# Cross-attention and FP4 feed-forward layer on one core: twenty loads of x issued by GpSimd instead of SyncE

## The chip, the core and the metric

One core of a Trainium2 chip runs the whole layer as one program. The metric is the device time of the program in microseconds (us), the median of several executions. The engines are called as the profile calls them: PE (TensorE), DVE (VectorE), ACT (ScalarE), POOL (GpSimd) and SP (SyncE, which here does nothing but issue DMA transfers). Each engine works through its own instructions in the order in which the program gives them; an instruction that has to wait for a semaphore holds up everything behind it on that engine.

## What is computed

The input `x` has 4 batches of 2048 rows of 512 numbers in float32; the context has 4 batches of 77 rows. Cut to what matters:

```python
def layer(x, ctx, mask, Wq, bq, Wk, bk, Wv, bv, Wo, bo, w_gate, w_up, w_down):
    x = x + attention(layernorm(x), ctx, ctx, mask, Wq, bq, Wk, bk, Wv, bv, Wo, bo)   # 16 heads of 32
    return x + ffn(layernorm(x), w_gate, w_up, w_down)

def ffn(x, w_gate, w_up, w_down):                    # widths 512 -> 1408 -> 512
    h = silu(fp4_linear(x, w_gate)) * fp4_linear(x, w_up)
    return fp4_linear(h, w_down)

def fp4_linear(x, w):                                # both operands rounded to 4-bit floats,
    return fp4(x) @ fp4(w).T                         # with one scale for each block of 16 numbers
```

The kernel does each product in float16 with two parts (high and low) of each operand, in three passes.

## The kernel before

The 8192 rows of `x` are worked on in 64 tiles of 128 rows. Before the tiles can run at full rate, the weights have to be loaded, scaled, rounded (gate, up and down weights: steps `wg0` to `wd3`) or split into two parts (attention weights, by PE products with scaled diagonals into PSUM and two ACT copies: steps `pk0` to `po3`), and keys and values of the context have to be made. Steps of the first tiles are woven into that preparation.

Every piece of work is a generator that yields its steps in order, and an emission order over all these steps is written out by hand in the string `INTRO` (the preparation and about the first eighteen tiles); after it a list of due times (`PLACE`) orders the steps, and a string `OUTRO` ends it. A word such as `at.8` in the string means "the next step of the attention of tile 8"; `at.2*2` means the next two. The order of the words is the order of the instructions on every engine. Moving an instruction to another engine does not change the string: the instruction keeps its place among all steps and so gets a new place among that engine's instructions.

Each tile `t` loads its 128 rows of `x` twice, 256 KB each time:

- `xin`, at line 875, the first step of `attention(t)`. There are two buffers, so the load of tile `t` waits until tile `t - 2` has been read for the last time, by DVE at line 887. The next steps of the tile are: moments of the rows on DVE (lines 845 and 847), five small POOL operations for the reciprocal standard deviation and a sixth for the bias `nb` (lines 853 to 860, 881), the normalised rows and their high part on ACT (883, 885), the low part on DVE (887), a transposing DMA (890), the query product on PE.
- `x`, at line 867, the first step of `residual(t)`; POOL then adds the output bias (869), and DVE adds the attention's output (1004). There are five buffers; at first some of them hold raw context and values of the preparation, later a buffer comes free when the tile that had it five tiles ago has been stored (1138).

Later steps of the attention that are named below: scores on PE (917), their masking and row maxima on DVE (928, 937), the negated maxima `nmx` on POOL (940), sixteen exponentials on ACT (944), the split of the probabilities on ACT and DVE (947, 949), a transposing DMA of them to `pT` (952), the product with the values on PE (969), its scaling on DVE (984, 987), a transposing DMA to `aT` (997), the output product on PE (1000). The feed-forward part of a tile follows with its products `gps`, `ups` and `dps`.

All DMA transfers of the kernel, loads, stores and transposes, are issued by SP, through one queue (q1 on the profile's page). The words of the order that surround five of the loads:

```
... sg at.0*3 pc0*4 dk pk1*2 v*3 dv pv2*2 pv1*2 pv2*2 pk1*2 at.1*3 pv0*2 wg0 wu2 wu1*2 ...
... wd2*3 wu3 sd*2 at.6*2 at.8 at.2*2 wd1 sd wd2 sd*2 wd1*2 at.0 ...
... at.1*2 r.1 at.0 gu.0 at.8 at.9*2 at.1*2 x.2 ...
```

In the first of these lines `at.0*3` is the load of tile 0, its moments on DVE and its six POOL operations; `dk` and `dv` (line 406, DVE) make the scaled diagonals that PE needs for the parts of Wk (`pk`) and Wv (`pv`). In the second, `sd` are scales of the down weights (line 757 on POOL, 781 on ACT, 784 on DVE), `at.6*2` is ACT's and DVE's preparation of tile 6 (883, 885, 887), `at.8` is the load of tile 8, and `at.2*2` is `nmx` of tile 2 on POOL and the first four of its exponentials. In the third, `r.1` are five POOL operations of tile 1 (line 1036), and `at.9*2` is the load of tile 9 and its moments.

Of the kernel before, what the change touches and what calls it, by code (L numbers as in the profile page):

```python
# [91 lines left out]
    x=(7.3299, 8.0685,),  # L92
    r=(8.1990,),
# [13 lines left out]
def step(e, take=(), give=(), wait=(), fire=(), on=False):  # L107


    return e, take, give, wait, fire, on  # L110
# [63 lines left out]
def tile_xattn_fp4_ffn(  # L174
# [18 lines left out]
    nc = tc.nc  # L193
# [3 lines left out]
    H, DK, P, Q = 16, 32, 128, 16  # L197
# [4 lines left out]
    ST = S // P  # L202
# [11 lines left out]
        x=5, xin=2, xhl=1, xT=2, qst=1, sc=1, pT=2, an=1, ahl=1, aT=1, xc=1, xqhl=1, xqT=2, sg=2, hh=2, ah=2, hqhl=1, hT=1, ax=1  # L214
    )

    def buf(tag, shape, dt, name=None):
        return wk.tile([P] + list(shape), dt, tag=tag, name=name or tag, bufs=BUFS[tag])
# [631 lines left out]
    def rstd(mv, k, f):  # L850
# [9 lines left out]
        nc.gpsimd.tensor_scalar(rs, e, r0, None, ALU.mult)  # L860
        return rs

    def residual(t):
        b, r = divmod(t, ST)
        yield step("D", take=[("x", t)], wait=[("vf", NB - 1)])
        xt = tiles["x", t] = buf("x", [D], F32)
        nc.sync.dma_start(xt, x[b].rearrange("(p t) d -> p t d", p=P)[:, r])
        yield step("G", wait=["bo"], fire=[("x", t)])
        nc.gpsimd.tensor_tensor(xt, xt, bo_sb, ALU.add)

    def attention(t):
        b, r = divmod(t, ST)
        yield step("D", take=[("xin", t)])
        xt = buf("xin", [D], F32)
        nc.sync.dma_start(xt, x[b].rearrange("(p t) d -> p t d", p=P)[:, r])
        yield step("V")
        mv = moments(xt, "1")
        yield step("G")
# [124 lines left out]
        xt = tiles["x", t]  # L1003
# [185 lines left out]
    def spawn(order):  # L1189
        while ("done", ended[0]) in order.events:  # L1190
            ended[0] += 1
        while begun[0] < min(N, ended[0] + AHEAD):
            t = begun[0]
            begun[0] += 1
            if t and t % ST == 0:
                order.add("kb", t, batch_keys(t // ST))
                order.add("vb", t, batch_values(t // ST))
            order.add("at", t, attention(t))
            order.add("x", t, residual(t))
            order.add("gu", t, gateup(t))  # L1200
            order.add("s", t, gates(t))
            order.add("r", t, second_rstd(t))
            order.add("px", t, scales_x(t))
            order.add("ph", t, scales_h(t))
            order.add("h", t, hidden(t))
        return begun[0] < N
# [43 lines left out]
```

## Time and profile before

| | |
|---|---|
| time, median of 3 runs | 2003.44 us (2000.14 to 2004.87) |
| the profiled execution's own time | 2004.46 us |
| its span, first to last instruction | 2002.7 us |
| busy: PE, DVE, ACT, POOL | 1892.5, 1714.4, 1385.5, 917.0 us |
| queue q1, all DMA transfers | 250.72 MB, 62.2% of 16 engines' span |
| issue of an `xin` load on SP, shortest, median, longest | 0.328, 0.571, 1.584 us |
| issue of an `x` load on SP, shortest, median, longest | 0.327, 0.328, 0.577 us |

In the views quoted below, an engine's row gives the start in us from the beginning of the span, the duration in us, the engine, the line of the kernel, the operation, what it writes and reads, shape and count, and in brackets the idle time of the engine before it with what ended it. "SPq" is an issue on SP: its duration is the time of the issue, not of the transfer. "PEclk" is the share of the full TensorE clock that was granted.

### The profile page before, as it was taken

What the parts mean: (1) busy time and instruction counts of PE and PEld (TensorE: products, weight loads), DVE (VectorE), ACT (ScalarE), POOL (GpSimd) and SP (SyncE); (2) the same over time, 40 slices, a digit from 0 to 9 for tenths busy, and PEclk for the clock granted to TensorE, in tenths of its full rate; (3) what the DMA queues carried; (4) which work ended last, traced back from release to release, by engine and by line L of the source; (5) the groups of instructions that cost most, each with busy time, mean ns of one, the idle gap of its engine ahead of it and who ended that gap; (6) DMA issues with size and microseconds to landing.
All of it is one profiled execution on the core that took longest, in us unless ns stands there. A gap on an engine that the chain in (4) does not pass through costs nothing.

```text
span 2002.7 us, 32553 instructions
## 1 busy us (share of the span) xinstructions
PE 1892.5 (94%) x11834; PEld 972.3 (49%) x11834; DVE 1714.4 (86%) x2810; ACT 1385.5 (69%) x2263; POOL 917.0 (46%) x1210
## 2 busy tenths in 40 slices
PE   2744999999999999999999999999999999999997
PEld 1622555555555555555555555555555555555543
DVE  7788988888888888898888888888889888888874
ACT  5867877667766777667766776677766776677531
POOL 4335345444444445544454445444454445444531
PEclk9866999999999999999999999999999999999999
DMA  8479676656656656665666575665765566656431
GB/s 251 91 198 206 105 136 127 130 120 125 133 121 131 122 122 125 132 120 121 129 129 118 123 130 119 132 126 116 135 131 114 120 128 128 119 117 114 88 76 45
DMA packets 778553, 252.80 MB, mean 126 GB/s; under 512 B 738292, under 2 KB 749684, under 8 KB 778391
## 3 DMA queue, kind: packets, MB, share of 16 engines
q1 hardware_dynamic: 778391, 250.72, 62.2%
q8 instruction: 92, 1.51, 0.3%
q14 instruction: 70, 0.57, 0.1%
HBM read 52.11 MB, written 17.92 MB: 35 GB/s over the span
## 4 chain that ended last, share of the span: by engine, by line
PE 88%; DVE 4%; ACT 3%; DMA 2%; POOL 1%; issue 1%; SPq 0%; DVEq 0%; POOLq 0%
PE dps L385 22%; PE gps L385 22%; PE ups L385 22%; PE ops L385 8%; PE qps L385 8%; PE avps L969 3%; PE scps L917 2%; PE wps L416 1%; ACT sc L944 1%; DMA hT<-hqhl 1%; DMA pT<-ph 1%; DMA wuT<-in_L_ffn_w_up_dram 0%; DVE wam L377 0%; DVE wsc L710 0%; DMA wdT<-wraw 0%
## 5 line engine op out<-in xcount | busy, mean ns | idle before, releaser
L385 PEld LDWEIGHTS <-xqT 128*128 128x128 f16 x4608 | 447.1, 98 | 453.9
L385 PE MATMUL ups<-wuT,xqT 128*128 128x512 f16 (+1 forms) x2304 | 487.8, 361 | 0.0
L385 PE MATMUL gps<-wgT,xqT 128*128 128x512 f16 (+1 forms) x2304 | 487.7, 361 | 0.0
L385 PE MATMUL dps<-wdT,hT 128*128 128x512 f16 x2112 | 468.4, 380 | 6.3 <-DMA hT<-hqhl 6.2
L944 ACT ACTIVATE sc<-sc,nmx,cells 128x77 f32<-128x77 f32 x1024 | 363.2, 438 | 8.6 <-POOL nmx L940 7.9
L385 PEld LDWEIGHTS <-hT 128*128 128x128 f16 x2112 | 206.8, 98 | 257.5 <-DMA hT<-hqhl 7.7
L1093 ACT ACTIVATE sg<-gps,cells 128x512 f32<-128x512 f32 (+1 forms) x192 | 123.8, 646 | 137.6 <-PE gps L385 133.0
L853 POOL TENSOR_SCALAR ve<-mv 128x1 f32<-128x1 f32 x128 | 111.1, 868 | 235.4 <-DVE mv L847 229.6
L385 PE MATMUL ops<-woT,aT 128*128 128x512 f16 x768 | 179.8, 384 | 17.3 <-DMA aT<-ahl 9.6
L704 POOL TENSOR_TENSOR hh<-hh,rh 128x1408 f32<-128x1408 f32 x64 | 165.7, 2589 | 42.8 <-DVE rh L764 42.3
L898 ACT ACTIVATE q<-qps 128x1024 f16<-128x1024 f32 x64 | 65.3, 1021 | 171.3 <-PE qps L385 171.3
L385 PE MATMUL qps<-wqT,xT 128*128 128x512 f16 x768 | 182.3, 389 | 0.0
L949 DVE TENSOR_TENSOR ph<-sc,ph 128x1232 f16<-128x1232 f32 x64 | 151.3, 2363 | 32.7 <-ACT ph L947 32.6
L883 ACT ACTIVATE xin<-xin,nb,rs 128x512 f32<-128x512 f32 x64 | 52.0, 813 | 173.5 <-POOL nb L881 173.5
L855 POOL TENSOR_TENSOR r<-ve,nhalf 128x1 f32<-128x1 f32 x128 | 153.5, 1199 | 10.7
L1103 DVE SCALAR_TENSOR_TENSOR hh<-ups,cells,sg 128x512 f32<-128x512 f32 (+1 forms) x192 | 128.5, 670 | 17.0 <-PE ups L385 15.3
L1069 POOL TENSOR_SCALAR cd<-pw,cells 128x1 f32<-128x1 f32 x64 | 18.3, 285 | 252.7 <-DVE pw L1066 252.7
L704 POOL TENSOR_TENSOR xc<-xc,rix 128x512 f32<-128x512 f32 x64 | 67.7, 1058 | 135.8 <-DVE rix L1020 130.3
L757 POOL TENSOR_SCALAR sh<-amh 128x88 f32<-128x88 f32 x64 | 33.3, 520 | 196.0 <-DVE amh L377 195.9
L385 PEld LDWEIGHTS <-xT 128*128 128x128 f16 x768 | 76.3, 100 | 87.5 <-issue 7.5
L385 PEld LDWEIGHTS <-aT 128*128 128x128 f16 x768 | 71.7, 99 | 96.6 <-DMA aT<-ahl 15.0
L857 POOL TENSOR_SCALAR e<-ve,r 128x1 f32<-128x1 f32 x128 | 102.7, 802 | 14.7
(190 smaller groups left out, 3023.3 us busy)
## 6 DMA issues: line engine op xcount, KB each, us to landing
xin<-in_x_dram SPq DMA_DIRECT2D x64, 256.0 KB
x<-in_x_dram SPq DMA_DIRECT2D x64, 256.0 KB
out_dram<-x SPq DMA_DIRECT2D x64, 256.0 KB
wgT<-in_L_ffn_w_gate_dram SPq DMA_DIRECT2D x4, 704.0 KB
wuT<-in_L_ffn_w_up_dram SPq DMA_DIRECT2D x4, 704.0 KB
wmraw<-in_L_ffn_w_down_dram SPq DMA_DIRECT2D x4, 704.0 KB
wraw<-in_L_ffn_w_down_dram SPq DMA_DIRECT2D x4, 704.0 KB
wqT<-in_L_xattn_Wk_dram SPq DMA_DIRECT2D x4, 256.0 KB
```

Source lines behind the costliest of these rows:

```text
L385: nc.tensor.matmul(o, lhs(a, c), rhs(b, c), start=(k == 0), stop=(k == 3 * n - 1))
L704: nc.gpsimd.tensor_tensor(dst.rearrange(blocks, j=Q), src.rearrange(blocks, j=Q), rinv.unsqueeze(2).to_broadcast([P, nb, Q]), ALU.mult)
L853: nc.gpsimd.tensor_scalar(ve, mv[:, 1:2], 1e-5, None, ALU.add)
L855: nc.gpsimd.tensor_tensor(r0, ve, nhalf, ALU.pow)
L857: nc.gpsimd.tensor_scalar(e, ve, r0, r0, ALU.mult, ALU.mult)
L883: nc.scalar.activation(xt, xt, AF.Identity, scale=rs, bias=nb_)
L898: nc.scalar.activation(q4[:, :, 0:3:2], q3.unsqueeze(2).to_broadcast([P, H, 2, DK]), AF.Copy)
L944: nc.scalar.activation(s3[:, h], s3[:, h], AF.Exp, scale=esc, bias=nm[:, h : h + 1])
L949: nc.vector.tensor_tensor(ph[:, 1, :SCW], sc, ph[:, 0, :SCW], ALU.subtract)
L969: nc.tensor.matmul(o[:, (lo - 8 * half_) * 33 : (hi + 1 - 8 * half_) * 33], pT[:rows, a * PC + c, :], vb[:rows, b_, c, (lo - CH0[c]) * 33 ...
L1093: nc.scalar.activation(sg, tiles.pop(("g", t, k)), AF.Silu, scale=cg[:, 0:1])
L1103: nc.vector.scalar_tensor_tensor(hh[:, c0 : c0 + n], tiles.pop(("u", t, k)), cg[:, 1:2], sg, ALU.mult, ALU.mult)
```

## The change

For tiles 0 to 9 both loads of `x` are issued by POOL (`nc.gpsimd`); tiles 10 to 63 keep SP. These are 20 of the 128 loads of `x`. Sources, destinations, buffers, sizes and the order of the steps are the same.

```diff
+    def fetch(t, dst):
+
+        b, r = divmod(t, ST)
+        (nc.gpsimd if t < 10 else nc.sync).dma_start(dst, x[b].rearrange("(p t) d -> p t d", p=P)[:, r])
+
     def residual(t):
         b, r = divmod(t, ST)
         yield step("D", take=[("x", t)], wait=[("vf", NB - 1)])
         xt = tiles["x", t] = buf("x", [D], F32)
-        nc.sync.dma_start(xt, x[b].rearrange("(p t) d -> p t d", p=P)[:, r])
+        fetch(t, xt)
...
         yield step("D", take=[("xin", t)])
         xt = buf("xin", [D], F32)
-        nc.sync.dma_start(xt, x[b].rearrange("(p t) d -> p t d", p=P)[:, r])
+        fetch(t, xt)
```

## Prediction

> **What bounds the kernel now.** I read the busy shares of PE in 40 slices first, then the chain of work that ended last, then a table by stages whose borders I chose from both.
>
> ```profile
> PE   2744999999999999999999999999999999999997
> PE 88%; DVE 4%; ACT 3%; DMA 2%; POOL 1%; issue 1%; SPq 0%; DVEq 0%; POOLq 0%
> ```
>
> ```profile
> 171.00:197.00 26.00, 13.62 (x86) 6.28 (x87) 22.01 (x33) 18.99 (x33) 15.13 (x17) 0.74 1.00 203
> 197.00:254.00 57.00, 57.00 (x398) 29.84 (x399) 51.03 (x87) 50.44 (x89) 19.38 (x35) 1.00 0.65 115
> 254.00:2002.70 1748.70, 1738.49 (x10806) 877.99 (x10802) 1511.01 (x2470) 1201.11 (x1942) 813.20 (x1060) 1.00 0.61 120
> ```
>
> The columns after the stretch are PE, weight loads, DVE, ACT, POOL (busy us and instructions), PEclk, DMA share, GB/s. From 197 us PE has no gap (57.00 of 57.00, then 1738 of 1749), and the chain is PE's for 88% of the span. So after 197 us a load counts only if it makes PE wait. Before 197 us PE waits for a chain over ACT, DVE, POOL and transfers. All 20 loads lie before 392 us, 13 of them before 171 us: the question is what they do to that first chain, which every later tile then inherits one for one.
>
> Three links of the chain, from the chain in order of time:
>
> ```profile
> 45.09 4.25 PE wps L416 x24
> 171.16 2.79 POOL nmx L940
> 190.11 6.83 DMA pT<-ph
> ```
>
> **What the change moves.** A load keeps its place among all steps, so on POOL it stands behind the POOL instruction emitted before it, and what POOL has next waits with it for the buffer. I laid the emission order beside the trace for each of the 20. Two numbers are not in the trace:
>
> - G, the time that POOL is held by issuing one load. Bounds: 0.33 us (the shortest such issue on SP) and 2.6 us (POOL's longest elementwise instruction, L704 on 128x1408). I take 1.0, near POOL's L704 on a tile of the same shape, 128x512 (1.06).
> - S, from the start of the issue to the reader's start. On SP: tile 9 196.30 to 199.51 = 3.2; tile 7 155.12 to 159.12 = 4.0; tile 6 135.09 to 139.70 = 4.6. The loads that matter run in quiet stretches, so 3.4; bounds 3.2 and 4.6.
>
> The Trainium skill, "DMA: Bandwidth & Descriptors", section "Anatomy of one DMA — SWDGE (gpsimd) path", fits a load from GpSimd as 2.0 us plus bytes over 436 GB/s; for 256 KB that is an estimate of 2.6 us, and S = 2.6 would take about 0.8 us off each of A and C below. No row here shows it.
>
> **A: tiles 0 and 1.**
>
> ```profile
> 32.56 1.01 SPq L875 DMA_DIRECT2D xin<-in_x_dram  x2
> ```
>
> ```profile
> 42.98 1.18 POOL L757 TENSOR_SCALAR sh<-wam 128x88 f32<-128x88 f32 x2
> 44.23 0.25 POOL L853 TENSOR_SCALAR ve<-mv 128x1 f32<-128x1 f32 x1
> 50.14 0.27 POOL L881 TENSOR_SCALAR nb<-mv,rs 128x1 f32<-128x1 f32 x1
> ```
>
> ```profile
> 42.72 0.68 DVE L845 BATCH_NORM_STATS2 st<-xin 128x6 f32<-128x512 f32 x1
> 43.44 0.18 DVE L847 BATCH_NORM_AGGREGATE mv<-st 128x2 f32<-128x6 f32 x1
> 43.54 0.25 DVE L406 TENSOR_SCALAR q<-ident,cells 128x128 f32<-128x128 f32 x1
> 54.05 1.63 DVE L710 SCALAR_TENSOR_TENSOR wsc<-wa,wsc 128x1408 f32<-128x1408 bf16 x1 [6.90 <-ACT wa L810]
> ```
>
> SP issues both loads at 32.6, ten us before DVE reads them. On POOL the load of tile 0 stands behind the two `sh` operations, which end at 44.16. It starts at 44.24, and DVE reads at 44.24 + 3.4 = 47.6 instead of 42.72. Behind that read on DVE is L406 (`dk`), the diagonal for the Wk parts: it ends at 47.6 + 0.9 + 0.25 = 48.8 instead of 43.79. PE began those products at 44.88, right before the link of 45.09; now 48.8, so +3.9. ACT's copies follow PE, then its L810, which released DVE's L710 at 54.05: now 57.9.
>
> Tile 1 joins: its load stands behind `nb` of tile 0, which needs the moments of tile 0 (48.5) and takes 2.35 us (the second group of six in the POOL view) to 3.75 (the first). So it issues at 51 to 52.4 and DVE reads at 54.4 to 55.8. Adding moments (0.9) and L719 (1.6), DVE reaches L710 at 56.9 to 58.3, against 57.9 from ACT: the 6.90 us of idle that cover this are just used up. A = +3.9. Bounds: 3.2 (an issue like SP's shortest, landed as tile 9's) to 6.7 (S = 4.6 in both loads).
>
> **Tiles 2 to 5: covered.** Each `xin` load now holds POOL until DVE's L887 of tile t-2 is done. Tile 2 waits inside a gap of 14.51 us (before 68.09). Tile 3 holds `sh` of 79.57 until L887 at 83.48; its reader on ACT (86.80) still gets it. Tile 4 holds `cells` (L532, 86.29) until L887 at 102.22 ends; its reader on ACT is at 110.98, and POOL otherwise waited 16.26 us there. Tile 5 holds four memsets and a `sh` (110.40 to 113.87, in all 3.5 us) until 113.49, before a gap of 5.33 us; with G = 1.0 that leaves 0.7, so zero, but G = 2.6 costs 0.9.
>
> **Tiles 6, 7 and the first `x` loads: small both ways.** Tile 6's load goes between `nmx` of tile 0 (ends 136.67) and L704 for the down weights: DVE reads at 140.15 instead of 139.70, and ACT's L810 waits G: +0.5. `x` of tile 3 is on the chain: POOL waits 11.87 us for it until 152.32. It can start when L601 has freed its buffer (146.92) and `x` of tile 2 is issued, 147.3, so L869 starts at 150.7: -1.6; the load of tile 7 (G) then stands before `sh`: -0.6 is left for ACT, of which DVE, with 0.21 us of idle at 162.73, can use 0.2. SP, rid of the issue of tile 5 at 113.5, loads a part of the down weights 0.6 earlier, where DVE waits 0.89 (127.23): -0.5. And L822 (156.41) no longer stands behind the load of tile 7 (1.2 us); DVE's L710 at 168.24, drawn out to 2.44 beside POOL's L704 (to 169.20), goes back towards 1.62: -0.8 at most, half of it taken in B. `x` of tile 0 costs a G before a wait of 0.8, `x` of tile 1 lands inside a gap of 6.19, `x` of tile 4 comes 11 us earlier and is read at 261. Together 0.5 - 0.2 - 0.5 = -0.2, bounds -1.5 and +1.
>
> **B: tile 8.**
>
> ```profile
> 169.29 1.78 POOL L757 TENSOR_SCALAR sh<-wamd 128x88 f32<-128x88 f32 x1
> 171.16 2.78 POOL L940 TENSOR_SCALAR nmx<-mx,cells 128x16 f32<-128x16 f32 x1
> ```
>
> ```profile
> 175.45 0.74 DVE L887 TENSOR_TENSOR xhl<-xin,xhl 128x512 f16<-128x512 f32 x1
> 178.01 1.63 DVE L719 TENSOR_TENSOR wraw<-wa,wraw 128x2816 f16<-128x2816 bf16 x1 [1.60 <-ACT wraw L715]
> 199.51 0.70 DVE L845 BATCH_NORM_STATS2 st<-xin 128x6 f32<-128x512 f32 x1 [1.30 <-DMA xin<-in_x_dram]
> ```
>
> On SP this load waited for L887 of tile 6 (ends 176.19) and went at 176.69. On POOL it stands between these two rows, so `nmx` of tile 2, ready and on the chain, waits for a buffer that it does not need: 176.19 + 0.08 + G 1.0 + 0.28 = 177.55, against 173.95. That is 3.6, less 0.4 for the quicker L710: B = +3.2. Behind `nmx`, ACT has the exponentials of tile 2, then the L715 that DVE's row at 178.01 waits for, then the probabilities whose transfer (190.11) starts the gapless PE at 196.98. Nothing in between has slack. Bounds: 2.1 (G = 0.33, all 0.8 of relief) to 5.2 (G = 2.6, none).
>
> **C: tile 9.** DVE already waits 1.30 for it, at 199.51. On POOL it stands behind the five operations of `r.1`, which end at 199.63; SP issued it at 196.30. With S 0.2 longer, DVE goes on 3.5 later. DVE's gaps until it hands over the first `hT` at 246.47 are 0.31, 0.43, 0.63 and 0.70, in sum 2.1, and PE takes `hT` at 254.06 without slack: C = 3.5 - 2.1 = +1.4, bounds 0 and 3.5.
>
> **`x` of tiles 5 to 9** (277 to 392 us): SP has already waited for the buffer when POOL gets there (up to 5 us later), POOL is idle 0.5 to 0.8 before the `nmx` that follows, and ACT begins the exponentials 1.7 us after that `nmx` ends (284.11 against 282.40). PE's gapless row hides the rest; were that cover gone it would cost 0.5 us a tile. Zero.
>
> Relief of SP: its 20 issues sum to 10.1 us, but only the 1.2 and 0.6 above end a wait. The Trainium skill, "DMA: Bandwidth & Descriptors", section "Issuing engines are not separate DMA queues", says that issuing from several engines saves only the issue time; by that rule alone the change could give at most these 10.1 us, 1993.3.
>
> **Sum.** 3.9 - 0.2 + 3.2 + 1.4 = +8.3 us on a span of 2002.7, so 2011.0, and an own time of 2004.5 + 8.3 = 2012.8. The profiled execution was 1.0 above the median, so the median goes to 2003.4 + 8.3 = 2011.7. A measurement here can tell about 0.2%, 4 us, from no change.
>
> **Rivals.**
> - *Relief decides (faster).* If the preparation's chain ran through SP alone, with POOL and DVE idle beside it, A and B would vanish in idle time and the gains stay: 1.6 at `x` of tile 3, 1.2 at L822, 0.5, 0.8: 4.1, so 1999.3. For it: the chain has the transfer of `x` (4.18 us from 147.98) in it. Against: it decides only if PE's parts have 3.9 us of slack after 44 us, and the link of 45.09 is on the chain. Chance 0.08.
> - *Hidden (no change).* A's delay is swallowed before 171 us by waits for transfers that do not move, and B shrinks to its lower bound 2.1, offset by the -1.5: 2003 to 2006. Chance 0.14.
> - *Dear issue (slower still).* G = 2.6 and S = 4.6: A 6.7, tile 5 0.9, B 5.2, C 1.4 + 1.2, others +1: 16.4, so 2019.8. For it: POOL's small operations are often drawn out to 1.5 or 2 us. Chance 0.18.
> - *The sum above:* 0.60.
>
> Range: the sum with A between 3.2 and 5, B 2.1 to 4.5, C 0 to 2.6 runs from +4 to +12; taking in part of the dear issue and of the hidden case it is 2004.5 to 2019. Faster by over 0.2% 0.07, within 0.2% 0.14, slower 0.79.
>
> **What would show it.** Right: the first L845 of DVE starts near 47.6 after some 4.8 us of idle released by the load; `nmx` of tile 2 starts over 3 us after its mx and right after a POOL issue that waited for L887; PE becomes gapless near 204 instead of 197; later stages last as before. Wrong: gapless PE still at 197 (then A and B were hidden), or POOL rows of over 2 us for an issue (dear issue), or a stage after 254 us that lasts longer.

## The result, and the profile after

The changed kernel takes 2021.14 us in the median of four runs (2017.45 to 2023.33), beside 2002.97 for the kernel before on the same chip. The ratio is 1.0085, 95% interval 1.0070 to 1.0101: slower by some 17 us (the medians are 18.2 apart). The prediction had 2011.7 and a range up to 2019.0: the sign was right, the predicted loss of 8.3 us was about half of the measured one, and the measured time lies above the range. The profiled execution has an own time of 2022.88 us and a span of 2021.1, 18.4 longer than before.

In the changed kernel the loads are line 866, and every later line that the prediction names has a number higher by 5 (887 is 892, 940 is 945, 969 is 974); 869, the bias on `x`, is 874.

The page's PE slices and chain, and the table by stages:

```profile
PE   1753899999999999999999999999999999999997
PE 85%; DVE 6%; DMA 3%; ACT 2%; POOL 1%; issue 1%; SPq 0%; DVEq 0%; POOLq 0%; ACTq 0%
```

```profile
171.00:197.00 26.00, 8.55 (x74) 4.45 (x71) 20.73 (x23) 14.97 (x20) 8.83 (x14) 0.78 0.74 157
197.00:254.00 57.00, 47.23 (x299) 23.43 (x297) 47.27 (x85) 42.64 (x79) 20.98 (x35) 0.86 0.71 136
254.00:2021.00 1767.00, 1756.36 (x10929) 887.57 (x10927) 1527.20 (x2492) 1218.60 (x1972) 822.17 (x1073) 1.00 0.61 120
```

Between 197 and 254 us PE was busy for 57.00 of 57.00 us before and is busy for 47.23 now. After 254 it lacks 10.6 us in 1767 (10.2 in 1749 before). So the whole loss lies in the first 254 us. Some of the longest links of the chain, in order of time, say where:

```profile
44.01 3.02 DMA xin<-in_x_dram
50.40 2.87 DMA xin<-in_x_dram
57.97 3.99 DVE wsc L710
...
111.21 8.48 DMA xT<-xhl
...
122.49 7.22 DMA wmraw<-in_L_ffn_w_down_dram
...
178.71 3.41 DVE wraw L710
...
214.76 3.08 DMA xin<-in_x_dram
```

Before, none of these stood among the longest links. Three are loads that POOL issues (tiles 0, 1 and 9), which the prediction expected. The transfer of `xT` that takes 8.48 us was not expected at all; the `wmraw` load at 122.49 stands on SP right behind the next transposition, which was late by it.

To follow the loss I take one instruction in both traces and subtract its starts: the lateness. Marks, with their starts before: L845 of tile 3 (105.51), `nmx` of tile 0 (136.39), `sh` right ahead of tile 8's load (169.29), L845 of `r.1` (196.51), L845 of tile 11 (301.57). Kernels that are still the same at a mark differ there by -1.5 to +2.0 us from one profiled execution to the other (both ends are in the tables below: e18 at 105.51, e5 at 169.29), so a single lateness below 2 us proves little. Each kernel has one trace, and it need not be a typical execution: that of e5 was the slowest of its 11 (2012.45 against a median of 2007.08), that of e7 one of its fastest (2005.44 against 2008.12).

| stretch between marks | predicted | measured, whole change |
|---|---|---|
| to 105.51: tiles 0 and 1 (A) | +3.9 | +4.58 |
| to 136.39: tiles 2 to 5, `x` of tiles 0 and 1 | 0 | +4.59 |
| to 169.29: tiles 6 and 7, `x` of 2 to 4 | -0.2 | +2.26 |
| to 196.51: tile 8 (B) | +3.2 | +3.44 |
| to 301.57: tile 9 (C) | +1.4 | +3.04 |
| sum | +8.3 | +17.91 |

A in the changed kernel, POOL first, then DVE:

```profile
42.85 1.10 POOL L757 TENSOR_SCALAR sh<-wam 128x88 f32<-128x88 f32 x2
44.01 0.76 POOL L866 DMA_DIRECT2D xin<-in_x_dram  x1
...
50.40 0.63 POOL L866 DMA_DIRECT2D xin<-in_x_dram  x1
...
57.88 2.59 POOL L704 TENSOR_TENSOR wsc<-wgT,rh 128x1408 f32<-128x1408 f32 x1
```

```profile
47.05 0.69 DVE L845 BATCH_NORM_STATS2 st<-xin 128x6 f32<-128x512 f32 x1 [4.38 <-DMA xin<-in_x_dram]
...
53.29 0.70 DVE L845 BATCH_NORM_STATS2 st<-xin 128x6 f32<-128x512 f32 x1 [4.15 <-DMA xin<-in_x_dram]
...
57.97 3.98 DVE L710 SCALAR_TENSOR_TENSOR wsc<-wa,wsc 128x1408 f32<-128x1408 bf16 x1 [2.26 <-POOL nb L886]
```

The load stands behind `sh`, DVE waits for it, and L710 starts at 57.97: the 57.9 of the prediction. But L710 then lasts 3.98 us instead of 1.63. POOL's L704, which reads two tiles, ran from 50.36 before, while DVE was idle:

```profile
50.36 2.59 POOL L704 TENSOR_TENSOR wsc<-wgT,rh 128x1408 f32<-128x1408 f32 x1
```

Now it starts 0.09 ahead of L710 and ends at 60.47, and L710 ends 1.48 after that. Across both traces, wherever L704 or the bias on `x` overlaps an L710 or L719 of this size on DVE, the DVE row is longer by about the overlap (0.96 of overlap, 2.44; 2.00, 3.48; 2.10, 3.60; 2.49, 3.98), and beside POOL's small TENSOR_SCALAR rows it stays at 1.62. The Trainium skill, "SBUF — State Buffer", section "SBUF: two separate sides", says that DVE and GpSimd share a pair of ports, that whoever starts first holds it for its whole instruction and that the other stands still. The rows beside L704 and the bias agree with that; beside POOL's small rows no DVE row of this size was drawn out, whichever started first.

B, the POOL rows:

```profile
187.86 0.58 POOL L866 DMA_DIRECT2D xin<-in_x_dram  x1 [5.37 <-DVE slh L784]
188.54 0.27 POOL L945 TENSOR_SCALAR nmx<-mx,cells 128x16 f32<-128x16 f32 x1
```

`nmx` of tile 2 stands right behind an issue that waited 5.37 us, as predicted. (The row names L784, the DVE row that ended last before it, at 187.78; L892 of tile 6, which frees the buffer, ended 0.21 earlier.)

The new link: the same ACT row, first after, then before:

```profile
119.77 0.63 ACT L890 ACTIVATE xhl<-xin 128x512 f16<-128x512 f32 x1 [3.30 <-DMA xT<-xhl]
```

```profile
111.92 0.63 ACT L885 ACTIVATE xhl<-xin 128x512 f16<-128x512 f32 x1
```

There is one `xhl` buffer. ACT may fill it for tile 3 when the transposition `xT` of tile 2 has read it. That transposition was issued 5.0 us later than before, and ACT is held 7.85. The DMA queues say what lay beside it: first a stretch before with transposes alone (packets, MB, share of 16 engines), then the stretch after in which POOL's queue q0 had the loads of `xin` of tile 4 and `x` of tile 0 under way:

```profile
DMA packets 2044, 0.52 MB, mean 258 GB/s; under 512 B 2044, under 2 KB 2044, under 8 KB 2044
...
q1 hardware_dynamic: 2044, 0.52, 119.2%
```

```profile
DMA packets 389, 0.32 MB, mean 108 GB/s; under 512 B 328, under 2 KB 328, under 8 KB 389
...
q0 software_dynamic: 74, 0.25, 82.5%
q1 hardware_dynamic: 315, 0.07, 17.6%
```

The first is 106 to 108 us, 1022 packets in a microsecond. The second is 113 to 116 us: 105 packets in a microsecond on SP's q1 beside the loads, and both together move 108 GB/s instead of 258. On the one queue they had run nearly in turn. Why the two queues together moved less than one of them alone is not shown by any run.

### The profile page after: what moved, and what is told of

Same layout as the page of the kernel before. It is cut to its first block, busy times and chain, and to the rows that moved or that the text cites. A ratio compares the mean times of both kernels' runs of the same rounds, so it can differ in the third digit from the quotient of the medians.

```text
span 2021.1 us, 32560 instructions
## 1 busy us (share of the span) xinstructions
PE 1894.7 (94%) x11834; PEld 974.2 (48%) x11834; DVE 1718.5 (85%) x2810; ACT 1385.5 (69%) x2263; POOL 921.2 (46%) x1230
## 4 chain that ended last, share of the span: by engine, by line
PE 85%; DVE 6%; DMA 3%; ACT 2%; POOL 1%; issue 1%; SPq 0%; DVEq 0%; POOLq 0%; ACTq 0%
PE dps L385 22%; PE ups L385 21%; PE gps L385 21%; PE ops L385 7%; PE qps L385 7%; PE avps L974 3%; PE scps L922 2%; DMA hT<-hqhl 1%; DMA xT<-xhl 1%; DMA pT<-ph 1%; ACT sc L949 1%; DVE wsc L710 1%; DMA xin<-in_x_dram 0%; DMA wuT<-in_L_ffn_w_up_dram 0%; PE wps L416 0%
## 5 line engine op out<-in xcount | busy, mean ns | idle before, releaser
L704 POOL TENSOR_TENSOR hh<-hh,rh 128x1408 f32<-128x1408 f32 x64 | 165.7, 2589 | 44.4 <-DVE rh L764 43.8
L954 DVE TENSOR_TENSOR ph<-sc,ph 128x1232 f16<-128x1232 f32 x64 | 150.6, 2353 | 32.3 <-ACT ph L952 32.3
L1074 POOL TENSOR_SCALAR cd<-pw,cells 128x1 f32<-128x1 f32 x64 | 18.2, 285 | 251.9 <-DVE pw L1071 251.9
L704 POOL TENSOR_TENSOR xc<-xc,rix 128x512 f32<-128x512 f32 x64 | 68.9, 1076 | 136.1 <-DVE rix L1025 132.2
```

Of the source, the lines that this page charges most:

```text
L704: nc.gpsimd.tensor_tensor(dst.rearrange(blocks, j=Q), src.rearrange(blocks, j=Q), rinv.unsqueeze(2).to_broadcast([P, nb, Q]), ALU.mult)
L954: nc.vector.tensor_tensor(ph[:, 1, :SCW], sc, ph[:, 0, :SCW], ALU.subtract)
```

## Experiments

All of them choose in `fetch` which loads POOL issues, by a line that replaces `t < 10` (`k` is "xin" or "x"); all other loads go by SP. Ratios are against the kernel before on the same chip, with 95% intervals.

```diff
-    def fetch(t, dst):
-
+    def fetch(t, dst, k):
+        pool = ...
-        (nc.gpsimd if t < 10 else nc.sync).dma_start(...)
+        (nc.gpsimd if pool else nc.sync).dma_start(...)
```

**One part at a time.**

```diff
+        pool = k == "xin" and t < 2                      # e1_first_two
+        pool = k == "xin" and 2 <= t < 6                 # e2_two_to_five
+        pool = (k, t) == ("xin", 8)                      # e5_eight
+        pool = (k, t) == ("xin", 9)                      # e6_nine
+        pool = k == "xin" and t in (6, 7)                # e7_six_seven
+        pool = k == "x" and t < 10                       # e8_x_only
```

> Only the xin loads of tiles 0 and 1 are issued by POOL; the other eighteen go by SP as before. The prediction's step A: +3.9 us alone, so about 2007 of a median of 2003 before, with the L710 step of wu1 starting at 57.9 and everything after it shifted by that. The theory after the trace of the whole change: +4.6, since L710 of wu1 (1.63 us before) runs 3.98 us where POOL's L704 of wg2 runs beside it, and this happens here too. Rival: the later gaps before hT absorb the delay of the first two tiles, so that less than 2 us is left at 260.

> Only the xin loads of tiles 2 to 5 are issued by POOL. The prediction's step called them covered: 0 us, 2003. The theory after the trace: the load of tile 4 and SP's transposes of the same time (qst of tile 0, xT of tile 2) are slow beside each other, so xT of tile 2 frees the one xhl buffer late, L890 of tile 3 waits some 3 us for it and the wmraw rows after it come late too: +2 to +4 us, first seen at L890 of tile 3 with DMA xT<-xhl as releaser. Rival: POOL's own order is the cause, L532 and the memsets L595 and L596 standing behind the load that waits for L892 of tile 2; then the delay is first seen on a reader of those and xT of tile 2 lands as soon after its issue as before.

> Only the xin load of tile 8 is issued by POOL, ahead of nmx of tile 2. The prediction's step B: +3.2 (nmx waits for L892 of tile 6, and the exponentials of tile 2 with it), 2006. Rival: the delay is real at nmx but is absorbed by the gaps before hT, so that under 1.5 us is left at the end; in the whole change it could not be absorbed since tile 9 added its own after it.

> Only the xin load of tile 9 is issued by POOL. The prediction's step C: 3.5 us late on DVE less 2.1 absorbed before hT, +1.4, 2004.5. In the whole change DVE was 3.48 later after this load and gave back only some 0.5 of it. If that holds alone: +3.0, 2006. If the absorption only failed because DVE was late there already by 14.9 us, it is +1.4 here.

> Only the xin loads of tiles 6 and 7 are issued by POOL. The prediction: +0.5 for tile 6 and nothing for tile 7, 2003.5. In the whole change DVE waited 4.98 us for the load of tile 6 and was 1.6 us later after it. If tile 6 costs that alone too, +1.6 to +2.6 and 2005; if its wait only stood in place of the lateness of the four tiles before, 0.

> Only the ten x loads are issued by POOL, all xin loads by SP. The prediction: relief of SP, -0.2 with bounds of -1.5 and +1, 2002 to 2004. The theory after the trace: x loads that run beside SP's transposes (x.0 of 111, x.3 of 157) slow these, so +0 to +2. Rival (Relief decides): with no xin load behind a wait on POOL, SP's queue is shorter where it ended waits, and this is the version that is faster than before, by 1 to 4 us.

| run | ratio | lateness at 105.51 | 136.39 | 169.29 | 196.51 | 301.57 |
|---|---|---|---|---|---|---|
| e1_first_two | 1.0029 (1.0018 to 1.0041) | 4.07 | 4.58 | 4.27 | 4.26 | 5.55 |
| e2_two_to_five | 1.0010 (1.0002 to 1.0019) | -1.10 | -0.56 | -0.17 | -0.17 | 1.33 |
| e7_six_seven | 1.0013 (1.0005 to 1.0022) | 0.67 | 0.13 | 1.04 | 1.04 | 0.88 |
| e8_x_only | 1.0010 (1.0001 to 1.0019) | 0.10 | -0.65 | 3.05 | 1.81 | 3.66 |
| e5_eight | 1.0016 (1.0007 to 1.0025) | 1.52 | 1.40 | 1.98 | 5.62 | 7.24 |
| e6_nine | 1.0009 (1.0000 to 1.0017) | 0.28 | 0.55 | 1.08 | 1.08 | 4.10 |

Tiles 0 and 1 alone cost about what the whole change loses on them (4.07 against 4.58), and nothing later swallows it (rival of e1 refuted). Here too L710 of `wu1` is drawn out, to 3.55. Tile 8 adds 3.64 between its two marks; its POOL rows repeat B:

```profile
178.43 0.78 POOL L866 DMA_DIRECT2D xin<-in_x_dram  x1 [5.38 <-DVE slh L784]
179.30 0.27 POOL L945 TENSOR_SCALAR nmx<-mx,cells 128x16 f32<-128x16 f32 x1
```

Tile 9 adds 3.0, as in the whole change and not the 1.4 of the prediction: lateness earlier on is not why C was larger. Tiles 2 to 5 alone add 0.5, which does not stand out of the spread, and L890 of tile 3 does not wait: my expectation of +2 to +4 was a miss, and so was the place where I expected to see it. Tiles 6 and 7 alone add about 1 us in the trace, no more than the spread; but that trace is of a fast execution, and 8 of the 11 took 2007.8 us or more. What those lost is in no trace. The `x` loads alone add 3.7 between 136.39 and 169.29 and give back 1.2: `x` of tile 4 goes 12 us earlier, beside SP's transposition of a down weight, the next part of the down weights is issued 1.5 us later, and POOL's L704 waits for it. They bring no gain, and the rival "Relief decides" is refuted. The six ratios add up to +0.87%, the whole change has +0.85%; the agreement is partly by chance, since the parts share a cost that is told below, with the clock.

**POOL's order without a transfer.**

```diff
+        if 2 <= t < 6: nc.gpsimd.memset(xt[:, 0:1], 0.0)    # ahead of SP's load, e3_hold
```

> All loads by SP; for tiles 2 to 5 POOL first sets one column of the xin buffer to zero, so that POOL waits for L892 of the tile two before, in the same place as in the changed kernel, with no transfer of its own. If POOL's order (the work queued behind that wait) costs the time of tiles 2 to 5, this is as slow as the kernel with the four loads on POOL, +2 to +4 us. If loads beside transposes cost it, this is within 1 us of before, 2003 to 2004.

Measured: ratio 1.0000 (0.9991 to 1.0008), lateness -1.7 at 169.29. That POOL waits for L892 in these four places costs nothing here, with tiles 0 and 1 on time. This half of the prediction's step was right.

**The two loads beside the transposition.**

```diff
+        pool = t < 10 and (k, t) not in (("xin", 4), ("x", 0))    # e4_but_at4_x0
+        pool = (k, t) in (("xin", 4), ("x", 0))                   # e9_at4_x0
```

> The whole change, but the xin load of tile 4 and the x load of tile 0 are left to SP. If these two beside the transposes hold up xhl of tile 3, the 3.3 us wait of L890 for DMA xT<-xhl goes and the kernel is 3 to 5 us faster than the whole change: 2016 to 2018. Rival: another wait takes its place (wmraw behind the two loads on SP, or the load of tile 5 on POOL), and it stays within 1.5 us of the whole change, 2020 to 2022. The prediction's own sum, with these two at zero, would have this kernel at the same time as the whole change.

> Only the xin load of tile 4 and the x load of tile 0 are issued by POOL. In the whole change both ran beside the transposes qst of tile 0 and xT of tile 2; xT was issued at 111.21 and its last packets started some 7.9 us later (2.7 before), and L890 of tile 3 waited 3.30 us for it. With either load alone on POOL the last packets started 4.8 us (tile 4) and 3.3 us (x of tile 0) after the issue, and L890 did not wait. Theory: two loads together are enough, whatever came before: L890 of tile 3 waits about 3 us with DMA xT<-xhl as releaser, +3 to +4.5. Rival: it takes the 4.6 us of lateness of tiles 0 and 1 as well (the loads then meet other transfers): no such wait here, 0 to +1.

Without the two, L890 of tile 3 no longer waits, and the lateness at 136.39 is 3.91 instead of 9.17; at 301.57 it is 13.42 instead of 17.91. The ratio is 1.0073 (1.0059 to 1.0087) against 1.0085 (1.0070 to 1.0101): the gain shows in the trace, the times alone (medians 2018.78 and 2021.14) don't separate the two kernels. The row that waited 3.30 us no longer waits:

```profile
115.57 0.63 ACT L890 ACTIVATE xhl<-xin 128x512 f16<-128x512 f32 x1
```

With only these two on POOL the wait comes back, smaller than I expected:

```profile
112.61 0.63 ACT L890 ACTIVATE xhl<-xin 128x512 f16<-128x512 f32 x1 [1.89 <-DMA xT<-xhl]
```

But it costs little: lateness -1.16 at 105.51 and -0.10 at 136.39, ratio 1.0007 (0.9998 to 1.0016). So the link is real (two loads beside the transposition make ACT wait, none or one did not), and its full price of 4.6 us arises only together with the lateness of tiles 0 and 1. That was the rival's point; the rival's "no such wait" was wrong.

**The same loads at other places of the written order.** The words moved, all in `INTRO`:

```diff
-... sg*2 ck*5 dc v q*4 ...  sg at.0*3 ...  pk1*2 at.1*3 ...
+... sg*2 ck*5 at.0 at.1 dc v q*4 ...  sg at.0*2 ...  pk1*2 at.1*2 ...      # tiles 0, 1: e10, e11
-... at.6*2 at.8 at.2*2 wd1 sd wd2 sd*2 wd1*2 at.0 at.7 at.4 ...
+... at.6*2 at.2*2 wd1 sd wd2 sd*2 wd1*2 at.0 at.7 at.8 at.4 ...            # tile 8: e11
-... at.7*2 px.0 ...  gu.0 at.8 at.9*2 ...
+... at.7*2 at.9 px.0 ...  gu.0 at.8 at.9 ...                               # tile 9: e11, e17, e18
+        pool = k == "xin" and t < 2          # e10_first_two_early
+        pool = t < 10                        # e11_all_placed
```

> The xin loads of tiles 0 and 1 are issued by POOL as in the change, but stand earlier in the written order, ahead of dc, so that POOL comes to them after its L704 of 30.71 to 33.30 and not after the two sh of 42.98. If A is the place in POOL's order and not the queue, DVE's first L845 is back at 42.7, the 4.6 to 4.9 us of A are gone: 0, within 1 us of before. Rival: the POOL queue itself is dear (issue to landing), and a part of A over 1 us stays.

> The whole change, all twenty loads on POOL, with four of them at other places of the written order: tiles 0 and 1 ahead of dc, tile 8 behind nb of tile 7 instead of ahead of nmx of tile 2, tile 9 right behind L892 of tile 7 instead of behind r.1. If A, B and C are places in POOL's order, this takes away 4.7 + 3.4 + 3.0 = 11 us of the 18: 2009 to 2011 where the whole change has 2021. Rival: the delays of tiles 2 to 7 grow when A is gone, or waits behind B and C take their place, and over 2014 is left.

The two loads of e10 go out at 33.03, and DVE's rows are those of before:

```profile
42.51 0.69 DVE L845 BATCH_NORM_STATS2 st<-xin 128x6 f32<-128x512 f32 x1
...
54.02 1.62 DVE L710 SCALAR_TENSOR_TENSOR wsc<-wa,wsc 128x1408 f32<-128x1408 bf16 x1 [7.08 <-ACT wa L810]
```

Lateness between -0.3 and +0.1 at every mark, ratio 1.0006 (0.9997 to 1.0014): A is the place in POOL's order, drawn-out L710 included, and not the queue. With all twenty loads on POOL and four of them moved (e11), the ratio falls to 1.0044 (1.0030 to 1.0058), 2012.96 us. Lateness: 0.06, 0.21, 3.44, 3.43, 8.60. So A and B are gone, and with A the 4.6 of tiles 2 to 5: L890 of tile 3 waits 2.03 us here and hardly any of it stays. The 3.2 of tiles 6, 7 and `x` stay. C did not go: with the early load of tile 9 the last stretch lost 5.2 us instead of 3.0, and PE waited 4.4 us for `pT` of tile 2.

**A pick of the loads that seemed harmless.** Tile 6's load was placed behind L892 of tile 4, tiles 8 and 9 as above.

```diff
+        pool = k == "xin" and t in (2, 3, 6, 8, 9)      # e12_pick
+        pool = k == "xin" and t in (2, 3, 6, 8)         # e16_pick_no_nine, tile 9 at its old place
```

> Only the xin loads of tiles 2, 3, 6, 8 and 9 are issued by POOL, that of tile 6 placed right behind L892 of tile 4, that of tile 8 behind nb of tile 7, that of tile 9 behind L892 of tile 7; the rest by SP. These are loads that the runs showed free of harm or harmful by their place only. If the waits of DVE for the loads of tiles 6 (4.35 us) and 9 (1.30 us) can be had back, -1 to -3 us, 2001 to 2003; if ACT's chain sets those times anyway, the same as before within 1 us.

> The pick with the load of tile 9 back on SP: POOL issues the xin loads of tiles 2, 3, 6 (right behind L892 of tile 4) and 8 (behind nb of tile 7). The pick was 2.58 us earlier than before at 198 us and lost 5.7 us there, where the load of tile 9 ran beside pT of tile 2 and PE waited 4.9 us for pT. Without that load: the 2.58 us stay, less up to 1.3 us that other runs lost near 205 us: 1 to 2.6 us faster than before, 2001.5 to 2003. If the loss comes from the earlier load of tile 8 or from the shift itself: slower than before by 1 to 3 us.

e12 has the ratio 1.0016 (1.0008 to 1.0025). It was 2.58 us early at 196.51 and 3.16 late at 301.57. In between PE waited for the transposition of tile 2's probabilities, for 1.6 us before, and in e12:

```profile
PE avps L974 <- DMA pT<-ph: 4.9, 1, 4.9
```

The load of tile 9, issued at 189.98, moved its packets from 194.2 to 196.9, beside those of `pT`. e16, without it, has 1.0009 (1.0000 to 1.0017) and a lateness of -0.11 at 196.51: the gain that I expected of it did not come. So the 2.58 were most likely spread (e3 shows -1.72 there), and no version tried here beats the kernel before.

**A load that nobody reads.** One more load of x (256 KB) into a tile of its own, near the transposition `pT` of tile 2, all others by SP:

```diff
+    idle = wk.tile([P, H * KV // 2], F32, tag="kst", name="idle", bufs=2)[:, :D]
+        if t == 7: nc.gpsimd.dma_start(idle, ...)    # behind L892 of tile 7, e13_beside_pool
+        if t == 2: nc.sync.dma_start(idle, ...)      # ahead of pT of tile 2, e14_before_sp
+        if t == 7: nc.scalar.dma_start(idle, ...)    # behind L892 of tile 7, e15_beside_act
```

> All twenty loads by SP as before, and one more load of x (256 KB) into a tile that nobody reads, issued by POOL near 188 us, in POOL's idle time, when SP's transposes wdT of wd2, then pT of tile 2 (190.11 to 194.90 before) are under way. It holds nobody and is waited for by nobody. If a load on POOL's queue beside SP's transposes slows them, PE's L974 of tile 2 starts 2 to 5 us later than before and the delay stays to the end: 2006 to 2009. If only its bytes count, 1.3 us at most. If the costs of the earlier runs came from places and buffers, 0.

> The same load that nobody reads, issued by SP itself right ahead of pT of tile 2: load and transposition in sequence on one queue. If queues beside each other are the trouble, this costs only the load's own issue and transfer, 0.6 to 2 us at PE's L974 of tile 2, so 2004 to 2006. If bytes near the transposition are the trouble, it costs as much as the load on POOL's queue.

> The same load that nobody reads, issued by ACT at about 191 us, while pT of tile 2 is under way. If any second queue slows the transposition, PE's L974 of tile 2 is 2 to 5 us late, as with POOL's queue. If it is POOL's queue alone, 0 to 1.3 us, and ACT is held only by the issue, some 0.5 us.

| run | ratio | PE's first product of `pT` later than L845 of `r.1` | longest wait of PE for `pT` |
|---|---|---|---|
| e13_beside_pool | 1.0009 (1.0000 to 1.0018) | 0.97 | 2.3 |
| e14_before_sp | 1.0004 (0.9995 to 1.0013) | 0.81 | 2.5 |
| e15_beside_act | 1.0019 (1.0009 to 1.0028) | 3.00 | 4.3 |

The third column is the lateness of that PE row less the lateness at 196.51. POOL's load was issued at 187.44, but its first packet moved at 190.25, when the transposes ahead of it were through, and its last at 192.6, before those of `pT`. So it did not test what it was made for, and 0.97 is no more than SP's own 0.81. The load of ACT did fall between the packets of `pT`; its queue is q10, from 194 to 198 us:

```profile
q1 hardware_dynamic: 1380, 0.35, 89.3%
q10 hardware_dynamic: 140, 0.26, 29.1%
```

345 packets in a microsecond on q1, where the same stretch of before (193 to 197 us) had 806, and PE 3.0 us late. SP had issued this `pT` on time, at 189.84 (190.11 before). So it is not POOL's queue as such: a load on another queue slowed a transposition where their packets mixed, and where they came in turn PE was late by 0.8 to 1.0 us, which does not stand out of the spread.

**One order, two queues.** The early place of tile 9's load alone:

```diff
+        pool = k == "xin" and t == 9      # e17_nine_early_pool
+        pool = False                      # e18_nine_early_sp
```

> Only the xin load of tile 9 is issued by POOL, at the early place (right behind L892 of tile 7), where it has nothing behind it on POOL that waits. If a load on another queue beside the transposition pT of tile 2 is the cause: PE's L974 of tile 2 waits 4 to 5 us for pT (1.6 before) and about +3 us stay, 2006 to 2008. If the loss of the pick came from its other loads: 0, or up to 1.3 us earlier, as DVE's wait for this load goes.

> The same written order, the load of tile 9 by SP, where it stands right behind pT of tile 2 on the one queue. If the queues beside each other are the cause, PE waits for pT as before (1.6 us), DVE's 1.30 us for the load shrink, and the time is that of before within 1 us or up to 1.3 us less. If the early place itself costs, it is as slow as the kernel with this load on POOL.

Ratios 1.0009 (1.0000 to 1.0018) and 1.0010 (1.0001 to 1.0019): the same. On POOL the load's packets came at 196.2 to 197.1, in one burst behind most of `pT`'s, and PE waited 2.1 us (2.4 in e18). So these two did not repeat the mixing of e12 either, and this pair decides nothing on it. What shows the price of mixing is the runs in which it happened: the whole change at 111 us, e12 and e15 at 194 us, e11 at 200 us. The same two instructions can mix or miss each other. (For e18, the other marks: -1.47 at 105.51, -0.52 at 196.51, 0.99 at 301.57.)

**The step near 205 us.** Nearly every other kernel lost 1.2 to 2.5 us between 196.51 and 301.57, e16 too, where no moved load is near (2.7 and more where tile 9 or a mixing came on top); e3, e7 and e10 lost nothing there. The windows of 4.00 us from PE's first product of `pT` (PE, weight loads, DVE, ACT, POOL, PEclk, DMA, GB/s) of before, e3, e10, e7, and then of e6, e14, e17:

```profile
196.98:200.98 4.00, 4.00 (x46) 2.49 (x47) 2.60 (x8) 3.65 (x8) 3.42 (x8) 1.00 1.11 224
```

```profile
195.28:199.28 4.00, 4.00 (x46) 2.48 (x47) 2.61 (x8) 3.66 (x8) 3.41 (x8) 1.00 1.01 225
```

```profile
196.77:200.77 4.00, 4.00 (x47) 2.46 (x48) 2.60 (x8) 3.62 (x8) 3.46 (x8) 1.00 1.01 224
```

```profile
197.82:201.82 4.00, 4.00 (x46) 2.48 (x47) 2.74 (x8) 3.63 (x8) 3.45 (x8) 1.00 1.04 225
```

```profile
198.04:202.04 4.00, 4.00 (x39) 2.48 (x40) 1.19 (x4) 3.65 (x8) 3.51 (x9) 0.57 0.87 160
```

```profile
198.26:202.26 4.00, 4.00 (x39) 2.56 (x40) 1.82 (x6) 4.00 (x10) 2.67 (x6) 0.57 1.02 223
```

```profile
197.92:201.92 4.00, 4.00 (x41) 2.23 (x42) 3.72 (x10) 4.00 (x10) 2.63 (x5) 0.68 0.77 133
```

The first four waited for `pT` 1.6, 1.4, 1.5 and 1.5 us, the last three 2.0, 2.5 and 2.1. In all twenty traces a wait of up to 1.6 us leaves the granted clock at 1.00 in the next 4 us, and a wait of 1.8 us (the whole change, 0.63) or more brings it to 0.50 to 0.68. The clock in these traces changes between 1.00 and 0.50 in steps of 3.41 us. The step that holds the wait and the step behind it, in before and then in e6:

```profile
194.89:198.31 3.42, 1.78 (x36) 1.32 (x35) 3.22 (x6) 0.98 (x1) 3.25 (x4) 1.00 1.10 223
198.31:201.72 3.41, 3.41 (x18) 1.54 (x16) 2.17 (x7) 3.41 (x10) 2.26 (x5) 1.00 0.94 198
```

```profile
195.22:198.63 3.41, 1.43 (x21) 0.79 (x20) 3.31 (x6) 0.24 (x1) 2.84 (x2) 1.00 1.13 235
198.63:202.05 3.42, 3.42 (x28) 1.89 (x26) 0.63 (x2) 3.42 (x8) 2.94 (x7) 0.50 0.83 156
```

In before PE was busy for 1.78 of 3.42 us and kept its clock, in e6 for 1.43 of 3.41 and had half of it for the next step. With one such step the stretch from PE's first product to ACT's copy of the queries of tile 5 takes 7.8 to 8.2 us where DVE is no later, instead of 6.9. The trace of before stands just above that edge, so that almost any disturbance costs 1.3 us once; the rest of those losses fits the later arrival of `pT` itself. No run sets the length of this wait alone. The Trainium skill, "TensorE: Matmul & The Clock Gate", section "What's actually happening", has the clock halved after an idle window of some 3.4 us; the length of the step agrees, but here PE was busy for 42% of it, and the measured number decides.

## Why the prediction was wrong, step by step

- **The cause in A and B was right.** G measured 0.54 to 0.78 us (1.0 taken), within its bounds. S was 2.9 to 3.1 for tiles 0, 1 and 9 (3.4 taken), just below its lower bound of 3.2; for `x` of tile 3 it was 5.03, above its upper bound of 4.6. "Dear issue" is refuted, since no issue took 2.6. L845 started at 47.05 after 4.38 of idle (47.6 and 4.8 said), L710 at 57.97 (57.9). B was 3.44 (3.2).
- **A's size** was 4.6 (4.1 in e1), not 3.9, a difference within the spread. What the step left out is that POOL's L704, no longer finished in DVE's idle time, would run beside L710: that drew L710 out by 2.35 us. The row behind it was 6.3 us late (61.98 against 55.71 before), and 4.6 of that were left at 105.51.
- **The step that failed is "Tiles 2 to 5: covered".** Its argument on POOL was right (e3: 0). It looked at what waits behind the load on POOL, and not at what the transfer runs beside. On SP's one queue load and transposition had come nearly in turn; on two queues they mixed, and both became slow (105 transposition packets in a microsecond instead of 1022). The zero became +4.6. e4 shows that the two loads are needed for it, e11 that A is needed too: 4.59 with A, at most 1.1 without it (e2 0.5, e9 1.1, e11 0.15).
- **Tiles 6, 7 and the first `x` loads**, -0.2 by sum, were +2.3. The gain of 1.6 at `x` of tile 3 did not come: its issue was 10.0 later than the one that the step had at 147.3, as was everything around it, but POOL's row then waited 4.49 us for the load, 5.03 from issue to reader where S = 3.4 was put in. Tile 6 cost 0.83 (lateness of `nmx` 9.17, of the L704 behind the load 10.00), near the 1.0 of G that the step charged to ACT. And `x` of tile 4 was no free relief (e8): in the whole change too, L704 of `wd2` waited 6.55 us for its weights.
- **C's size** was 3.0, not 1.4. DVE was 3.48 us later, as said (3.5). The 2.1 us of gaps did not give it back. ACT took up 1.5 of it (lateness 14.97 to 16.97), but then POOL's L704 for `xc`, 1.06 us before, started 0.14 behind a DVE row that reads two tiles (L954, 225.47 to 226.91), lasted 2.22, and ACT behind it was 17.9 late:

```profile
225.61 2.22 POOL L704 TENSOR_TENSOR xc<-xc,rix 128x512 f32<-128x512 f32 x1 [0.41 <-DVE slx L1052]
```

The halved clock of that stretch ("The step near 205 us") ran beside this: ACT's copy of the queries followed without a gap on a row that had waited 1.9 us for DVE. Kernels without a late tile 9 lose 1.2 to 1.5 us there (e9, e1, e2), so C and the clock share this stretch, and the parts do not simply add up.

- **Gapless PE near 204** was wrong, since PE meets `pT` of tile 2 with a lateness of 14.9 and not of 7: it comes at 212, and in 197 to 254 us PE lacks 9.8 us. The stages after 254 us were right.
- **Hidden** is refuted: A and B are there in full at 301.57 us.
- **Relief of SP** was worth nothing measurable in any run, well below the 10.1 us that the rule quoted in the prediction allows. The same section of the skill says that transfers of all issuers interleave on the same engines; it gives no price for that, and the prediction put none.

What stays open: why the mixing at 111 us costs 4.6 only when tiles 0 and 1 are late. In the whole change the two loads fell into one stretch with the transposition (105 packets in a microsecond on q1), in e9 the load of tile 4 trickled beside it (410), and behind L890 some 2 us of waiting were absorbed (1.89 in e9, 2.03 in e11), 3.30 were not. Which packets meet was not put under control by any run, and why mixed packets are slow is open too. For tiles 6 and 7, the times of e7 say more than its trace shows.

## What to carry to other kernels

Before moving a transfer to another issuing engine, list three things: what it now stands behind and holds up in that engine's order, what the transfer runs beside once it no longer stands in turn with the rest, and which instruction pairs on DVE and POOL slide over each other through the shift. The first could be repaired here by another place in the order (e10 took A to zero), the other two can't be read from busy shares. And parts that cost nothing alone can cost several us together, so a "covered" step has to be checked with the lateness of the steps before it.

## What the runs showed of the hardware

- Transposes alone moved 1022 packets in a microsecond (before, 106 to 108 us). With two loads of POOL's queue beside them it was 105 (the whole change, 113 to 116 us), with one load of ACT's queue 345 (e15, 194 to 198 us). The loads slow down too: the time from issue to landing of POOL's `xin` loads in the whole change was 2.9 us at the least, 3.6 in the median, 10.1 at the most.
- POOL was held 0.54 to 0.78 us by the issue of a 256 KB load. In e13 the first packet moved 2.8 us after the start of the issue, when the transposes ahead were through.
- Near 200 us a PE wait of up to 1.6 us left the granted clock at 1.00, one of 1.8 us or more brought it to 0.50 to 0.68 over the next 4 us, worth about 1.3 us once. The clock changed in steps of 3.41 us.
- DVE's L710 and L719 (1.62 us) were drawn out by about the time that they shared with POOL's L704 or the bias on `x`, up to 3.98 us; beside POOL's small TENSOR_SCALAR rows they were not.
